# Rows of exponentials kept in DRAM and loaded spread, in place of a transpose and an exponential per target tile

## The chip, the cores and the metric

The kernel runs on one core of one Trainium2 chip. The metric is the time of one execution on the device, in microseconds. Three runs of the kernel before took 1933.40, 1940.33 and 1942.73 us; the median is 1940.33 us.

## The reference

Two graph attention layers work on 3,327 nodes with 1,024 features each and a sparse 0/1 adjacency matrix (each node has some 16 neighbours and itself). Each layer is followed by a residual sum and a layer norm:

```python
x = _layernorm(x + _L0_gnn_ref(x, adj, W, a_src, a_dst))   # 8 heads of 128
x = _layernorm(x + _L1_gnn_ref(x, adj, W, a1, a2))         # one head, relu

# layer 1
h = input @ W
f1 = h @ a1
f2 = h @ a2
e = leaky_relu(f1 + f2.T, negative_slope=0.2)
scores = where(adj > 0, e, -9e15)
attention = softmax(scores, axis=1)
h_prime = attention @ h
return relu(h_prime)
```

The weight of a source j for a target i is exp(leaky_relu(f1[i] + f2[j])). The softmax is free to scale each target's weights by a common factor, so the kernel divides by exp(0.2 f1[i]) and works with max(exp(0.8 f1[i]) * exp(f2[j]), exp(0.2 f2[j])). For each target it needs one number, exp(0.8 f1[i]), and for each source two, exp(f2[j]) and exp(0.2 f2[j]).

## The kernel before

The nodes are padded to 26 tiles of 128 (NT = 26). The program first projects all tiles for layer 0 and lists the edges of each target tile. Then one written sequence of 52 items follows, made by `pipeline`: 26 items `Layer0` and 26 items `Target` (layer 1). Under `tc.manual_schedule()` every engine runs its instructions in the order of the program text, so what stands ahead in an engine's queue is done first. Waits are set where two instructions touch the same tile.

*Blocks.* A target tile has its edges in up to five blocks: four blocks of four groups of 32 targets each, and a fifth (`EB`) for what is left over. For every block, `gather` (L1011) has POOL issue indirect DMAs (L1017), one for each group, which bring 128 source rows into one of five buffers (`near` and `src`; two further ones, `end`, for the fifth block). A target thus takes 17 gathers. `send()` issues the next gather as soon as PE has finished with the buffer it goes into.

*A target of layer 1.* `weights(b)` (L1216) makes the 128 x 128 weights of a block on DVE in three passes: the row of the target's exponentials times the source's number (L1223), the maximum with the source's other number (L1224), times the one-hot marks (L1226). The first two results lie in PSUM, in the tile `way`. `sums(b)` (L1229) multiplies the weights with the gathered rows on PE (L1235). The weights of a block are made while PE works on the block before it. `close` divides by the sum of weights on ACT and DVE. `finish` transposes the result on PE (L196, copied by ACT at L199), multiplies it with W (L1267, 32 matmuls of 512 columns) and adds the residual (L1270). `settle` is the layer norm (L217 to L224, with ACT's square root at L220) and the store to `out` (L1278). `pipeline` cuts `finish` and `settle` of the one or two targets before into steps and puts them between the blocks of the current one.

*The exponentials of the target.* The scores f1 of all nodes are in the columns `r1.s` (one column of 128 partitions for each tile), written at the end of layer 0. `Target.prepare` of the next target is called in the middle of the current target (ahead of block 2's sums, j == nb // 2). PE transposes the column, spread over 128 columns, into `way` (L1191), so that each partition holds the whole row of 128 scores; ACT makes the exponentials of it in another part of `way` (L1193), and DVE reads them from there in L1223. Then `prepare` has DVE make the marks (L1033, L1037) and SP load the target's own row of y (L1198). `own` (L1200) makes the weight of the target's own node and needs the exponentials as a column: ACT makes them at L1204, DVE uses them at L1205.

*The end of a tile of layer 0.* `Layer0.finish` normalises the tile, makes both scores (L1168), has ACT put the two exponentials of the source score into the row (L1173, L1174) and SP store it in `y_d` (L1175). The gathers of layer 1 read `y_d`.

SP issues all plain loads and stores, POOL the gathers. The 16 DMA engines carry both.

Of the kernel before, what the change touches and what calls it, by code (L numbers as in the profile page):

```python
# [9 lines left out]
F32 = mybir.dt.float32  # L10
# [3 lines left out]
AF = mybir.ActivationFunctionType  # L14
OP = mybir.AluOpType
# [4 lines left out]
P = 128  # L20
SLOPE = 0.2
# [5 lines left out]
def kernel(  # L27
# [28 lines left out]
    nc = tc.nc  # L56
    N, D = x.shape
    H, DH = a0_src.shape
    NT = (N + P - 1) // P
# [10 lines left out]
    NG = P // GT  # L70
# [37 lines left out]
    scratch = ctx.enter_context(tc.tile_pool(name="scratch", bufs=1, space=DRAM))  # L108

    ident = const.tile([P, P], F32, name="ident")  # L110
# [14 lines left out]
    idx = const.tile([P, NT, NB], I32, name="idx")  # L125
    tgt = const.tile([P, NT, NB], F32, name="tgt")
    wt1 = const.tile([P, KT, D], F32, name="wt1")
    half_d = [scratch.tile([P, D], F32, name=f"half_d{t}") for t in range(EARLY)]
    dens = const.tile([P, EARLY, H], F32, name="dens")
    io_t = const.tile([P, P], F32, name="io_t")  # L130
# [41 lines left out]
    class Phase:  # L172
# [12 lines left out]
        def bank(self, tag, shape, name, dt=F32):  # L185
            psum, bufs = self.banks[tag]
            return psum.tile(shape, dt, tag=tag, name=name, bufs=bufs)

        def sbuf(self, tag, shape, bufs, name=None, dt=F32):
            return self.pool.tile(shape, dt, tag=tag, name=name or tag, bufs=bufs)  # L190
# [319 lines left out]
    with ExitStack() as own, tc.manual_schedule():  # L510
        ph = Phase(own, "proj", {"A": 2, "T": 1})
        pool, bank = ph.pool, ph.bank
# [389 lines left out]
        tr = bank("T", [1, P], "trc")  # L902
# [50 lines left out]


    def sparse(own):
        ph = Phase(own, "sparse", {"A": 4, "S": 2, "T": 1, "E": 1})
        pool, bank, sbuf = ph.pool, ph.bank, ph.sbuf
        NS = 5
        srcs = near + [pool.tile([P, NG, HG], F32, bufs=1, name=f"src{n}") for n in range(HB, NS)]
        ends = [pool.tile([P, 1, HG], F32, bufs=1, name=f"end{n}") for n in range(2)]  # L960
        r1 = Rows(pool, 1)

        ys = [pool.tile([P, HW], F32, bufs=1, name=f"y{n}") for n in range(3)]
        for y in ys:
# [3 lines left out]
        way = bank("E", [P, HALF], "way")  # L968
# [59 lines left out]
        def marks(t):  # L1028

            m = NB - 1  # L1030
            oh = sbuf("oh", [P, m * GT + P], 2)
            parts = oh[:, : m * GT].rearrange("p (b t) -> p b t", t=GT), oh[:, m * GT :]
            nc.vector.tensor_tensor(  # L1033
                parts[0], io_t[:, :GT].unsqueeze(1).to_broadcast([P, m, GT]),
                tgt[:, t, :m].unsqueeze(2).to_broadcast([P, m, GT]), OP.is_equal,
            )
            nc.vector.tensor_scalar(parts[1], io_t, tgt[:, t, m:], None, op0=OP.is_equal)  # L1037
            return parts

        class Layer0:  # L1040
# [9 lines left out]
            def prepare(self):  # L1050
                self.re = listed.pop(self.t)
                self.oh, self.oh2 = marks(self.t)
                self.y = ys[self.n % 3]
                load_rows(self.y[:, :D], x, self.t)
                self.h = sbuf("own", [P, HW0], 2)
                nc.sync.dma_start(self.h, h0_d[self.t * P : (self.t + 1) * P, :HW0])
                if self.t < EARLY:
                    self.half = sbuf("xT", [P, KT, P], 2, "half").rearrange("p k q -> p (k q)")
                    nc.sync.dma_start(self.half, half_d[self.t])

            def own(self):

                t, h = self.t, self.h
                es = self.es = sbuf("es0", [P, H], 2)
                nc.scalar.activation(es, sd0[:, t, 0, :], AF.Exp, scale=1 - SLOPE)
                nc.vector.tensor_tensor(es, es, h[:, D : D + H], OP.mult)
                nc.vector.tensor_tensor(es, es, h[:, D + H :], OP.max)
                nc.vector.tensor_scalar(es, es, loop[:, t : t + 1], None, op0=OP.mult)
                for n in range(H):
                    d = slice(n * DH, (n + 1) * DH)  # L1070
                    if t < EARLY:
                        nc.vector.scalar_tensor_tensor(
                            h[:, d], h[:, d], es[:, n : n + 1], self.half[:, d], op0=OP.mult, op1=OP.add
                        )
                    else:
                        nc.scalar.activation(h[:, d], h[:, d], AF.Copy, scale=es[:, n : n + 1])  # L1076
                if t < EARLY:
                    nc.vector.tensor_tensor(es, es, dens[:, t, :], OP.add)
# [69 lines left out]
            def finish(self):  # L1148

                met = sbuf("met", [NG * H, P], 2)  # L1150
                nc.vector.tensor_tensor(met, self.den[: NG * H, :P], meets, OP.mult)
                nc.tensor.matmul(self.den[:, P:], met, heads, start=True, stop=True)
                yield
                ri = sbuf("ri", [P, H], 2)
                nc.vector.tensor_tensor(ri, self.den[:, P:], self.es, OP.add)
                nc.vector.reciprocal(ri, ri)
                t, row = self.t, self.y
                y = row[:, :D]
                for h in range(H):
                    yh = y[:, h * DH : (h + 1) * DH]  # L1160
                    nc.vector.scalar_tensor_tensor(
                        yh, self.acc[h // 4][:, h % 4, :], ri[:, h : h + 1], yh, op0=OP.mult, op1=OP.add
                    )
                yield
                yield from ph.norm_steps([y])
                for n in range(2):
                    pr = sbuf("pr", [P, D], 1)
                    nc.vector.scalar_tensor_tensor(  # L1168
                        pr, y, 1.0, wa[n], op0=OP.mult, op1=OP.mult, accum_out=r1.sd[:, t, n, :]
                    )  # L1170
                    if n == 0:
                        yield
                nc.scalar.activation(row[:, D + 1 : D + 2], r1.d[:, t, :], AF.Exp)  # L1173
                nc.scalar.activation(row[:, D + 2 : D + 3], r1.d[:, t, :], AF.Exp, scale=SLOPE)  # L1174
                nc.sync.dma_start(y_d[t * P : (t + 1) * P, :HW], row)  # L1175
                stored.add(t)

        class Target:
# [8 lines left out]

            def prepare(self):
                t = self.t
                tr = way[:, 3 * P :]  # L1190
                nc.tensor.transpose(tr, r1.s[:, t, :].to_broadcast([P, P]), ident)  # L1191
                self.r = way[:, ((t + 1) % 2) * P : ((t + 1) % 2 + 1) * P].rearrange("p (g t) -> p g t", g=NG)
                nc.scalar.activation(  # L1193
                    self.r.rearrange("p g t -> p (g t)"), tr, AF.Exp, scale=1 - SLOPE
                )
                self.oh, self.oh2 = marks(t)
                self.res = ys[self.n % 3]
                nc.sync.dma_start(self.res, y_d[t * P : (t + 1) * P, :HW])  # L1198

            def own(self):  # L1200

                t, res = self.t, self.res
                es = self.es = sbuf("es1", [P, 2], 2)
                nc.scalar.activation(es[:, 1:], r1.s[:, t, :], AF.Exp, scale=1 - SLOPE)  # L1204
                nc.vector.scalar_tensor_tensor(  # L1205
                    es[:, 1:], res[:, D + 1 : D + 2], es[:, 1:], res[:, D + 2 : D + 3], op0=OP.mult, op1=OP.max
                )
                nc.vector.tensor_tensor(es[:, :1], es[:, 1:], loop[:, t : t + 1], OP.mult)

# [284 lines left out]
    with arm.Else():  # L1494
        with ExitStack() as own:
            sparse(own)
# [23 lines left out]
```

## Time and profile before

| What | Value |
|---|---|
| median of three runs | 1940.33 us |
| profiled execution, its own time | 1945.79 us |
| its span, first to last instruction | 1944.1 us |
| mean granted TensorE clock | 0.918 |
| PE busy | 1633.7 us (84%) |
| DVE busy | 1184.5 us (61%) |
| ACT busy | 573.4 us (29%) |
| POOL busy | 1092.2 us (56%) |
| L1193 ACT, the exponentials of 26 rows | 262 ns each |
| L1191 PE, the transposes of 26 columns | 272 ns each |
| L1204 ACT, the exponentials of a column | 187 ns each |

Layer 0's items run until about 1190 us, layer 1's from there to the end. A profile row gives line, engine, operation and tile names, then the shapes; "<-" in brackets names what ended the idle time ahead of the instruction. An engine's busy share is a mean over stages with different limits, so the stage windows and the waits say more than the page's first line. "Granted clock" is the share of full speed that TensorE was given.

### The profile page before, as it was taken

The numbers are of one execution on the slowest core, as the hardware profiler recorded it, in microseconds if no ns is written. First come the engines' busy times: TensorE is split into PE (matmuls) and PEld (weight loads), VectorE is DVE, ScalarE is ACT, GpSimd is POOL, SyncE is SP. The second block draws the span as 40 slices with busy tenths as digits, with TensorE's granted clock in tenths as the row PEclk, the third lists the DMA queues.
The fourth block names the chain that finished last, engine by engine and source line by source line (L and its number), as shares of the span: only waits on it lengthen the run. The fifth ranks groups of instructions, "written<-read, shape, count | busy, mean of one in ns | idle before, by whom it ended". The sixth has DMA issues, their size and how long they took to land.

```text
span 1944.1 us, 35431 instructions
## 1 busy us (share of the span) xinstructions
PE 1633.7 (84%) x13168; PEld 919.9 (47%) x13168; DVE 1184.5 (61%) x3261; ACT 573.4 (29%) x1565; POOL 1092.2 (56%) x1580
## 2 busy tenths in 40 slices
PE   8699989989994777777777665798989999899988
PEld 5466556655563554554455442243434434333433
DVE  6699988777765776777777774243444344434342
ACT  5656554444321222222222121022122221222121
POOL 4433346656555666666666555565656666565640
PEclk9899999999996878888878877899999999999999
DMA  6555779887779999999999998899999999899980
GB/s 178 91 130 114 144 152 293 255 249 238 247 271 349 381 391 393 383 393 371 402 386 386 374 313 301 310 374 340 346 350 369 335 394 342 331 362 340 325 302 33
DMA packets 183364, 585.16 MB, mean 301 GB/s; under 512 B 36168, under 2 KB 42824, under 8 KB 183182
## 3 DMA queue, kind: packets, MB, share of 16 engines
q0 software_dynamic: 131056, 457.74, 68.4%
q1 hardware_dynamic: 52126, 125.06, 17.2%
q8 instruction: 107, 1.75, 0.4%
q14 instruction: 75, 0.61, 0.1%
HBM read 586.09 MB, written 51.22 MB: 328 GB/s over the span
## 4 chain that ended last, share of the span: by engine, by line
PE 43%; issue 10%; DVE 6%; ACT 4%; DMA 4%; POOL 1%; another core or an unknown queue 0%; DVEq 0%; ACTq 0%; POOLq 0%
PE mm L1267 17%; PE acc L1235 13%; PE acc L1129 8%; PE acc L1110 2%; DMA src<-h_d,idx 2%; PE tr L196 1%; ACT L1193 1%; PE acc L1118 1%; DVE e L1098 1%; ACT own L1076 1%; DMA near<-h_d,idx 1%; DVE pr L982 1%; DVE st L217 1%; ACT L220 1%; DMA src<-y_d,idx 1%
## 5 line engine op out<-in xcount | busy, mean ns | idle before, releaser
L542 PE MATMUL mm<-wt,xT 128*128 128x347 f32 (+1 forms) x1248 | 416.6, 475 | 6.8 <-ACT ht L561 3.3
L1267 PE MATMUL mm<-wt,xT 128*128 128x512 f32 x832 | 395.5, 613 | 2.6 <-issue 2.3
L1017 POOL DMA_INDIRECT src<-y_d,idx x248 | 249.1, 1005 | 166.8 <-PE acc L1235 71.0
L542 PEld LDWEIGHTS mm<-wt,xT 128*128 128x128 f32 x1248 | 228.5, 195 | 118.3 <-issue 19.7
L1017 POOL DMA_INDIRECT src<-h_d,idx x184 | 196.5, 1068 | 121.3 <-PE acc L1129 35.8
L1267 PEld LDWEIGHTS mm<-wt,xT 128*128 128x128 f32 x832 | 152.3, 193 | 211.5 <-issue 206.7
L1270 DVE SCALAR_TENSOR_TENSOR o<-mm,y 128x512 f32<-128x512 f32 x52 | 36.0, 692 | 322.2 <-PE acc L1235 126.4
L1017 POOL DMA_INDIRECT near<-y_d,idx x168 | 169.5, 1009 | 108.7 <-PE acc L1235 48.3
L1129 PE MATMUL acc<-src,e 128*32 128x128 f32 x2944 | 161.3, 324 | 52.1 <-issue 47.5
L1017 POOL DMA_INDIRECT near<-h_d,idx x120 | 130.6, 1088 | 82.4 <-PE acc L1129 31.0
L1235 PE MATMUL acc<-src,es 128*32 128x341 f32 x1488 | 130.6, 485 | 41.8 <-DVE es L1226 31.8
L1129 PEld LDWEIGHTS acc<-src,e 128*32 128x32 f32 x2944 | 111.5, 130 | 113.4 <-issue 93.8
L1098 DVE TENSOR_TENSOR e<-oh,way 128x1024 f32<-128x1024 f32 x104 | 127.1, 1222 | 59.3 <-ACT w L1096 43.1
L1129 PE MATMUL acc<-near,e 128*32 128x128 f32 x2048 | 116.0, 333 | 48.7 <-issue 34.8
L199 ACT ACTIVATE xT<-tr 128x512 f32<-128x512 f32 x104 | 62.1, 598 | 299.9 <-PE tr L196 151.6
L1129 PEld LDWEIGHTS acc<-near,e 128*32 128x32 f32 x2048 | 79.7, 133 | 93.7 <-issue 84.4
L1096 ACT ACTIVATE w<-way 128x32 f32<-128x32 f32 x104 | 20.3, 195 | 351.4 <-DVE way L1094 186.6
L1249 ACT ACTIVATE z<-y,ri 128x342 f32<-128x342 f32 (+1 forms) x78 | 39.5, 569 | 277.0 <-issue 121.6
L1235 PE MATMUL acc<-near,es 128*32 128x342 f32 (+1 forms) x1008 | 85.8, 469 | 21.3 <-DVE es L1226 14.0
L629 POOL DMA_INDIRECT near<-h_d,idx x76 | 82.1, 1080 | 31.5 <-issue 22.9
L1235 PEld LDWEIGHTS acc<-src,es 128*32 128x32 f32 x1488 | 44.4, 114 | 115.0 <-issue 61.1
L346 ACT ACTIVATE junk<-ad 128x1664 uint8<-128x1664 uint8 x52 | 83.8, 1611 | 16.2 <-POOL ad L342 14.8
(242 smaller groups left out, 2587.8 us busy)
## 6 DMA issues: line engine op xcount, KB each, us to landing
h_d<-ht SPq DMA_DIRECT2D x26, 520.0 KB
own<-h_d SPq DMA_DIRECT2D x26, 520.0 KB
y_d<-y SPq DMA_DIRECT2D x26, 514.0 KB
y<-y_d SPq DMA_DIRECT2D x26, 514.0 KB
x<-in_x_dram SPq DMA_DIRECT2D x25, 512.0 KB
y<-in_x_dram SPq DMA_DIRECT2D x25, 512.0 KB
out_dram<-o SPq DMA_DIRECT2D x25, 512.0 KB
ad<-in_adj_dram POOLq DMA_DIRECT2D x25, 415.9 KB
```

What stands on the lines that cost most here:

```text
L199: nc.scalar.activation(part, tr, AF.Copy)
L346: nc.scalar.activation(junk, ad[:, n * THR : (n + 1) * THR], AF.Copy, accum_out=self.d[:, n : n + 1])
L542: nc.tensor.matmul(acc, xT[t][:, k, :], wt[:, k, CUTS0[c] : CUTS0[c + 1]], start=k == 0, stop=k == KT - 1)
L629: nc.gpsimd.indirect_dma_start(out=src[n % 3][:, g, :], out_offset=None, in_=h0_d[:THR, :], in_offset=bass.IndirectOffsetOnAxis(ap=idx[:, ...
L1017: nc.gpsimd.indirect_dma_start(out=s[:, g, :w], out_offset=None, in_=table[:n, :], in_offset=bass.IndirectOffsetOnAxis(ap=idx[:, t, b * NG ...
L1098: nc.vector.tensor_tensor(e, oh.unsqueeze(2).to_broadcast([P, ng, H, wide]), wp.unsqueeze(3).to_broadcast([P, ng, H, wide]), OP.mult,)
L1110: nc.tensor.matmul(self.acc[j - 1].rearrange("p h d -> p (h d)"), ident, self.h[:, (j - 1) * HALF : j * HALF], start=False, stop=False,)
L1129: nc.tensor.matmul(self.acc[h // 4][g * GT : (g + 1) * GT, h % 4, :], e[:, g, h, :], rowsof[:, g, h, :], start=first and h % 4 == 0, stop= ...
L1235: nc.tensor.matmul(self.acc[c][to, :m], es[:, g, :], s[:, g, CUTS[c] : CUTS[c + 1]], start=b == 0, stop=b == EB,)
L1249: nc.scalar.activation(z[:, cut], self.res[:, cut], AF.Copy, scale=ri[:, 1:2])
L1267: nc.tensor.matmul(acc, xT[:, k, :], wt1[:, k, half], start=k == 0, stop=k == KT - 1)
L1270: nc.vector.scalar_tensor_tensor(o[:, half], acc, 0.0, res[:, half], op0=OP.max, op1=OP.add)
```

## The change

At the end of a tile of layer 0, ACT makes the exponentials of the target score as a column too, in a column of the new tile `grow`, and SP stores these 128 numbers in a DRAM tile of their own (`row_d[t]`), one number from each partition. `Target.prepare` has no transpose and no exponential left: SP loads the 128 numbers into all 128 partitions of a new SBUF tile `rr` (two buffers), each partition reading the same 512 bytes. `own` reads the column from `grow`. The row of exponentials so lies in SBUF where it lay in PSUM.

```diff
+    row_d = [scratch.tile([1, P], F32, name=f"row_d{t}") for t in range(NT)]
...
+        grow = pool.tile([P, NT], F32, bufs=1, name="grow")
...
                 nc.scalar.activation(row[:, D + 1 : D + 2], r1.d[:, t, :], AF.Exp)
                 nc.scalar.activation(row[:, D + 2 : D + 3], r1.d[:, t, :], AF.Exp, scale=SLOPE)
+                nc.scalar.activation(grow[:, t : t + 1], r1.s[:, t, :], AF.Exp, scale=1 - SLOPE)
                 nc.sync.dma_start(y_d[t * P : (t + 1) * P, :HW], row)
+                to = row_d[t][:, :]
+                nc.sync.dma_start(
+                    bass.AP(tensor=to.tensor, offset=to.offset, ap=[[1, P], [1, 1]]), grow[:, t : t + 1]
+                )
...
             def prepare(self):
                 t = self.t
-                tr = way[:, 3 * P :]
-                nc.tensor.transpose(tr, r1.s[:, t, :].to_broadcast([P, P]), ident)
-                self.r = way[:, ((t + 1) % 2) * P : ((t + 1) % 2 + 1) * P].rearrange("p (g t) -> p g t", g=NG)
-                nc.scalar.activation(
-                    self.r.rearrange("p g t -> p (g t)"), tr, AF.Exp, scale=1 - SLOPE
+                self.r = sbuf("rr", [P, P], 2).rearrange("p (g t) -> p g t", g=NG)
+                of = row_d[t][:, :]
+                nc.sync.dma_start(
+                    self.r.rearrange("p g t -> p (g t)"),
+                    bass.AP(tensor=of.tensor, offset=of.offset, ap=[[0, P], [1, P]]),
                 )
...
                 es = self.es = sbuf("es1", [P, 2], 2)
-                nc.scalar.activation(es[:, 1:], r1.s[:, t, :], AF.Exp, scale=1 - SLOPE)
                 nc.vector.scalar_tensor_tensor(
-                    es[:, 1:], res[:, D + 1 : D + 2], es[:, 1:], res[:, D + 2 : D + 3], op0=OP.mult, op1=OP.max
+                    es[:, 1:], res[:, D + 1 : D + 2], grow[:, t : t + 1], res[:, D + 2 : D + 3], op0=OP.mult, op1=OP.max
                 )
```

## The prediction

> **What bounds the kernel now.** I read the page first (shares by engine), then the windows by stage, then the waits of layer 1 and last the timeline of one target in it. The page has PE busy for 84% of the span, but its busy rows are not the limit everywhere. The windows, whose columns are stretch, length, busy us of PE, PEld, DVE, ACT and POOL, granted clock, DMA share and GB/s, separate the stages:
>
> ```profile
> 660.00:1180.00 520.00, 387.89 (x5228) 259.50 (x5220) 383.22 (x1005) 120.67 (x331) 323.11 (x304) 0.84 0.99 379
> 1276.73:1881.22 604.49, 557.18 (x3147) 238.85 (x3147) 244.57 (x727) 128.42 (x220) 376.85 (x376) 0.98 0.94 350
> 1441.92:1466.67 24.75, 24.75 (x147) 10.78 (x151) 11.89 (x36) 5.84 (x10) 14.94 (x15) 1.00 0.88 325
> 1548.70:1602.85 54.15, 49.47 (x287) 21.35 (x287) 22.21 (x66) 11.67 (x20) 35.93 (x37) 1.00 1.01 393
> ```
>
> The first is layer 0: the DMA engines are full (0.99), PE is not. The second is layer 1, 22 targets at 604.49/22 = 27.48 us each: PE is busy for 557.18 and idle for 47.3, and the DMA engines have 6% left. The third is the one target in which PE never waits: 24.75 us. What ends PE's idle time between 1276 and 1882 is in the waits (total us, times, longest):
>
> ```profile
> DVE way L1223 <- ACT way L1193: 53.2, 16, 3.4
> PE acc L1235 <- DVE es L1226: 44.6, 19, 2.8
> ```
>
> PE waits for DVE's weights, and DVE for ACT's exponentials at L1193. One occurrence, in the timeline:
>
> ```profile
> 1517.55 0.60 ACT L199 ACTIVATE xT<-tr 128x512 f32<-128x512 f32 x1 [7.18 <-PE mm L1267]
> 1518.17 1.28 ACT L220 ACT_TABLE_LOAD   x1
> 1519.46 0.20 ACT L220 ACTIVATE sg<-sg 128x1 f32<-128x1 f32 x1
> 1519.68 1.28 ACT L1193 ACT_TABLE_LOAD   x1
> 1520.98 0.26 ACT L1193 ACTIVATE way<-way 128x128 f32<-128x128 f32 x1
> ...
> 1516.96 0.68 DVE L1033 TENSOR_TENSOR oh<-io_t,tgt 128x512 f32<-128x512 f32 x1
> 1517.56 0.28 DVE L1037 TENSOR_SCALAR oh<-io_t,tgt 128x128 f32<-128x128 f32 x1
> 1521.27 0.30 DVE L1223 TENSOR_TENSOR way<-way,near 128x128 f32<-128x128 f32 x1 [3.44 <-ACT way L1193]
> ...
> 1515.86 3.70 PE L1267 MATMUL mm<-wt,xT 128*128 128x512 f32 x8
> 1522.28 3.59 PE L1235 MATMUL acc<-near,es 128*32 128x341 f32 x24 [2.73 <-DVE way L1224]
> ```
>
> ACT swaps its function table twice per target, for the square root (L220) and back for the exponential. DVE starts 0.03 us after ACT ends, though this L1223 makes block 3 of the current target and L1193 makes the row of the next one: both lie in the tile "way", so the wait is on the tile, not on the value. PE then stands for 2.73 us, and its next 24 matmuls take 3.59 us where 1.93 is usual, at half clock.
>
> **Removed.** (1) L1193, the last use of that tile by ACT, and with L1204 the last exponential of layer 1. The square root then finds its table loaded, so 22 + 22 loads of 1.28 us go in this window; ACT is 21% busy (128.42 of 604.49), so that time by itself is worth nothing. What counts is that L1223 no longer follows ACT. In the occurrence above DVE is free at 1517.84; 0.30 + 0.30 + 0.29 us of work with the gaps of the rows give the weights at about 1518.85, and PE needs them at 1519.56. Next late is DVE's own chain, with 0.7 us to spare. PE's period falls to the third window's 24.75: 22 x (27.48 - 24.75) = 60.0 us, of which 47.3 is idle time and 557.18 - 22 x 24.75 = 12.7 is half clock. To it come 1.5 us (the stall at 1276.73, before the window) and 1.4 us (half clock behind the stall at 1881.22).
> (2) L1191 on PE, 0.27 us, of which little is exposed: from the four transposes to the sums behind them is 0.64 us start to start with it and 0.53 without; 26 x 0.11 = 2.9 us. PE's side in all: 60.0 + 1.5 + 1.4 + 2.9 = 65.8 us.
>
> **Added.** (3) In layer 0 one more ACT exponential per tile, 0.19 us like L1174, behind what the store of y waits for; ACT is 23% busy there. DVE at L1205 reads the stored column and waits for nothing new. (4) Per tile a store of 128 words on SP's queue, behind the store of y and ahead of the next tile's loads: an issue of 0.32 us on a queue that issues about five times in some 20 us. These are 128 packets per tile in a stage whose DMA is full. The nearest rows are loads of 4-byte words between 252 and 256 us, and one 544-byte set between 341 and 342 (packets, MB, share of 16 engines):
>
> ```profile
> q1 hardware_dynamic: 1233, 0.00, 17.3%
> q1 hardware_dynamic: 144, 0.07, 23.8%
> ```
>
> The first gives 0.173 x 16 x 4.0/1233 = 9 ns each: 26 x 128 x 9/16 = 1.9 us. No row shows a store of single words; the far bound is the page's mean packet of that queue, 0.172 x 16 x 1944.1/52126 = 103 ns, which makes 21 us. I take 2, since size is what the price follows in the two lines. (5) Per target a load of 128 packets of 512 bytes; the second line, 0.24 us of all engines, gives 26 x 0.24 = 6.2 us, 5.2 in the window. On SP it stands ahead of the load of y and behind the out store of the tile before. It waits only for that and for the buffer of the target before last: it can go out at about 1496 for weights made at 1530. The row y_d to y goes out at 1515.47 and is needed by 1533.67, without a wait shown. Cover: some 20 us; beyond that each us of lateness is a us of PE. (6) The row now lies in SBUF, so L1223 reads two SBUF operands. DVE L1033 reads two as well, and POOL's issue beside it took the usual time, while a fast single-operand pass stretched one:
>
> ```profile
> 1516.73 0.99 POOL L1017 DMA_INDIRECT src<-y_d,idx  x1 [0.31 <-issue]
> 1522.09 1.18 POOL L1017 DMA_INDIRECT src<-y_d,idx  x1 [0.30 <-DVE way L1224]
> ```
>
> So nothing (no gain either: DVE's passes L1223 to L1226 take 0.29 to 0.30 us wherever their operands lie), with an upper bound of the whole of L1223: 5 x 0.30 = 1.5 us of POOL per target. POOL's work is 17 x 1.30 = 22.1 us per target, so even 23.6 stays under 24.75. The Trainium skill (GPSIMD Engine Reference, Specifications) says that GpSimd's SBUF interfaces meet contention from Vector instructions with two SBUF inputs; by it the upper bound would hold. This trace shows none beside L1033.
>
> **What limits the gain: the gathers.** The 22 periods moved 350 GB/s. At layer 0's sustained 379 they take 604.49 x 350/379 = 558 us, at the 393 of the fourth window 538, at share 1.00 of their own mix 568; with the added rows (5.2) that saves 41, 61 or 31 us. On top comes the lead: the last gather is issued at 1883.80, its sums start at 1912.59, 28.8 us later, of which about 6 is transfer (issue stops at 1503.87, the engines' share drops after 1509). Up to 23 us may be used up over the layer: DMA's side allows 54 to 84 us, PE's side 65.8 - 1.9 = 64. Two limits so near each other rarely both hold in full, since each slip of one stalls the other; I take 55, DMA's low end.
> The Trainium skill (DMA: Bandwidth & Descriptors, Specifications) puts the HBM limit of one core at about 358 GB/s, which speaks against the change: as an estimate, 604.49 x 350/358 = 591 us, a saving of 13 us before the lead. The 379 over 520 us in the first window is above that, so the measurement decides.
>
> **Sum.** The profiled execution took 1945.79 us, with a span of 1944.1 and 1.7 around it: 1945.79 - 55 = 1891. It stands 5.5 above the median shown, 1940.33, so I forecast 1940.33 - 55 = 1885.
>
> **Rivals.**
> B. The gathers bound layer 1 from the start and no lead is used: saving 31 to 41, 1899 to 1909. For it: share 0.99 and 1.01 in whole stretches already. Against: in the unstalled target it is 0.88, and POOL waits 94 us (56.0 + 38.3) for PE to free buffers, so transfers aren't what PE waits for.
> C. DVE's chain takes the stall's place. It has 0.7 us; if L1270 ahead of it comes 2 us later, half the stall is back: saving about 30 less little, 1905 to 1922. For it: L1270 itself waits for PE, in the same order as before.
> D. The change doesn't do what it says: another wait on ACT or on the loaded row ends at the same time. Then only L1191's 2.9 less 1.9 is left: 1935 to 1945. Against: the 0.03 us between L1193 and L1223.
> E. Slower: PE, now in step with the gathers, idles often in short pieces and falls to half clock, as in layer 0, where the mean is 0.84. At that clock 24.64 us of work take 29.3, 1.85 more than now: + 41 us, 1981. It decides where layer 1's mean clock falls under 24.64/27.48 = 0.90. For it: after the gather wait of 8 us at 1236 PE ran slowly until 1257. Against: PE had 25% idle in layer 0 and would have some 5% here.
>
> **How the numbers follow.** My forecast 0.55 (own range 1872 to 1898), B 0.20, C 0.13, D 0.05, E 0.07. Range 1868 (PE's side with all of DMA's) to 1922 (C's end), leaving out D, E and a little more. About 0.5%, 10 us, is what this kernel's measurement tells from no change: faster is A, B and C, 0.88; same 0.05; slower 0.07.
>
> **What would show it.** Right: no table loads in layer 1 but one, no wait of L1223 on ACT, periods of 25 to 25.5 us, DMA share 0.98 or more, a few waits of L1223 on gathers late in the layer. Wrong: periods above 27, a mean clock under 0.9, L1223 waiting on the load of the row, or layer 0 longer by more than 5 us.

## The result, and the profile after

The changed kernel is slower. Six runs took 2010.01 to 2023.93 us with a median of 2013.69; beside them, six runs of the kernel before took 1927.85 to 1953.39 with a median of 1941.53. The ratio is 1.038, with a 95% interval of 1.033 to 1.043 (the medians alone give 1.037). The forecast was 1885 us, with a range up to 1922 and a chance of 0.07 for slower.

The profiled execution took 2017.74 us, with a span of 2015.4 us: 71.3 us more span than before. Where layer 1's sums begin divides it. These are the first rows of the sums line before (L1235) and after (L1241); behind the duration stand the first and last start:

```profile
L1235 PE MATMUL acc<-src,es x1488: 447/451/779, 1198.0 to 1899.0; 128*32 128x342 f32 x124, 128*32 128x341 f32 x62
```

```profile
L1241 PE MATMUL acc<-src,es x1488: 447/451/779, 1311.7 to 1970.0; 128*32 128x342 f32 x111, 128*32 128x341 f32 x75
```

What comes ahead of layer 1's sums grew by 1311.7 - 1198.0 = 113.7 us; what follows shrank from 1944.1 - 1198.0 = 746.1 to 2015.4 - 1311.7 = 703.7, by 42.4 us. The gain is there, and a loss more than twice as large stands in front of it. The stage windows of the changed kernel (columns as in the prediction) show both:

```profile
660.00:1180.00 520.00, 332.35 (x4372) 232.39 (x4366) 318.53 (x832) 100.23 (x291) 261.32 (x252) 0.75 1.01 311
1311.70:1394.30 82.60, 55.91 (x333) 20.71 (x333) 22.39 (x72) 6.91 (x12) 46.52 (x47) 0.82 0.85 296
1394.30:1952.90 558.60, 556.42 (x3125) 243.28 (x3124) 242.28 (x727) 63.72 (x132) 372.44 (x374) 1.00 1.00 381
```

The last line is layer 1's 22 regular targets: 558.60/22 = 25.39 us each, where they took 27.48 before. PE is idle for 2.2 us of them (before: 47.3) at a clock of 1.00, and ACT's busy time has halved. The groups by line on ACT show why. L221, L220 before, is the square root of the layer norm of both layers: its loads went from 50 to 27, one for each tile of layer 0 and one more at 1391.69 us, ahead of the regular targets. The 23 loads of the exponential in layer 1 (L1193) are gone. First two rows of the kernel before, then all loads of the changed kernel:

```profile
L220 ACT ACT_TABLE_LOAD x50 | 64.2, 1283 | 1.0
L1193 ACT ACT_TABLE_LOAD x23 | 29.5, 1283 | 0.4
```

```profile
L221 ACT ACT_TABLE_LOAD x27 | 34.6, 1283 | 0.8 <-issue 0.4
L1175 ACT ACT_TABLE_LOAD x26 | 33.4, 1283 | 0.6 <-issue 0.2
L200 ACT ACT_TABLE_LOAD x1 | 1.3, 1283 | 0.8 <-PEq L1514 0.8
```

The first line of the stage windows is the loss. In layer 0 the DMA engines are as full as before (1.01 against 0.99), but move 311 GB/s where they moved 379. One tile shows how. Its word store is issued at 702.85 us; these are windows of 2 us:

```profile
706.00:708.00 2.00, 0.18 (x1) 0.18 (x2) 1.41 (x2) 0.32 (x2) 1.21 (x2) 0.83 1.00 409
708.00:710.00 2.00, 2.00 (x4) 0.81 (x4) 1.63 (x4) 0.20 (x1) 0.99 (x1) 0.50 1.06 409
710.00:712.00 2.00, 2.00 (x33) 1.54 (x36) 1.93 (x9) 0.00 (x0) 0.00 (x0) 0.50 1.28 80
712.00:714.00 2.00, 2.00 (x42) 1.80 (x35) 1.30 (x4) 0.00 (x0) 0.00 (x0) 0.50 0.94 84
714.00:716.00 2.00, 2.00 (x22) 1.01 (x24) 0.00 (x0) 0.00 (x0) 0.99 (x1) 0.96 1.35 136
716.00:718.00 2.00, 0.89 (x24) 0.47 (x17) 0.00 (x0) 0.00 (x0) 0.84 (x1) 1.00 1.23 162
718.00:720.00 2.00, 0.57 (x3) 0.25 (x3) 0.00 (x0) 0.00 (x0) 1.14 (x2) 1.00 0.28 64
720.00:722.00 2.00, 0.94 (x10) 0.51 (x13) 0.40 (x2) 0.05 (x1) 0.00 (x0) 0.75 0.99 385
```

Read the last two columns together. Up to 710 us the 16 engines are full and move 409 GB/s. For the next 8 us they are booked as full or more and move 80 to 162, then they are nearly idle for 2 us, and at 720 they are back at 385. Packets are open all the while and hardly end. They are not the store's own: its packets of 4 bytes start between 708.2 and 710.1 us and are recorded with 9 ns each. The gathers' packets of 4,160 bytes, nearly all of which take 161 ns between 700 and 708 us, are held up behind them: of the 208 that start between 710 and 718 us a quarter take 0.94 us or more, the longest 4.75. Over the tiles the loss is 113.7/26 = 4.4 us per tile. A share of 1.00 thus says that packets are under way, not that bytes are moving; only the GB/s beside it shows the stall.

The last such store also stands in the turn from layer 0 to layer 1. Layer 1's gathers read what was stored just ahead of it, and the profile names the store of the words as the end of POOL's wait:

```profile
1311.07 0.32 SPq L1178 DMA_DIRECT2D y_d<-y  x1
1311.48 0.38 SPq L1180 DMA_DIRECT2D row_d<-grow  x1
1311.92 0.78 SPq L1199 DMA_DIRECT2D rr<-row_d  x1
1320.78 0.98 POOL L1019 DMA_INDIRECT src<-y_d,idx  x1 [23.71 <-DMA row_d<-grow]
```

POOL starts 9.7 us after that tile's store of y was issued. Before the change it was 1201.18 - 1197.37 = 3.8 us, and what ended the wait there was PE, not a store:

```profile
1201.18 0.99 POOL L1017 DMA_INDIRECT src<-y_d,idx  x1 [14.12 <-PE acc L1235]
```

### The profile page after: what moved, and what is told of

Same layout as the page of the kernel before. It is cut to its first block, busy times and chain, and to the rows that moved or that the text cites. A ratio compares the mean times of both kernels' runs of the same rounds, so it can differ in the third digit from the quotient of the medians.

```text
span 2015.4 us, 35459 instructions
## 1 busy us (share of the span) xinstructions
PE 1639.4 (81%) x13142; PEld 940.2 (47%) x13142; DVE 1184.0 (59%) x3261; ACT 506.5 (25%) x1493; POOL 1081.3 (54%) x1580
## 4 chain that ended last, share of the span: by engine, by line
PE 41%; DMA 17%; issue 6%; DVE 4%; POOL 1%; ACT 1%; SPq 0%; DVEq 0%; another core or an unknown queue 0%; POOLq 0%; ACTq 0%
PE mm L1273 18%; PE acc L1241 12%; DMA src<-h_d,idx 10%; PE acc L1131 5%; DMA near<-h_d,idx 2%; PE acc L1112 2%; DMA end<-h_d,idx 2%; PE acc L1120 1%; DMA own<-h_d 1%; PE tr L197 1%; DVE e L1100 1%; DVE pr L984 1%; POOL src L1019 1%; DMA src<-y_d,idx 1%; DMA half<-half_d 1%
## 5 line engine op out<-in xcount | busy, mean ns | idle before, releaser
L1019 POOL DMA_INDIRECT src<-h_d,idx x184 | 189.7, 1031 | 204.2 <-PE acc L1131 72.0
L1131 PEld LDWEIGHTS acc<-src,e 128*32 128x32 f32 x2944 | 120.5, 143 | 147.8 <-issue 84.0
L1241 PE MATMUL acc<-src,es 128*32 128x341 f32 x1488 | 135.6, 468 | 27.9 <-DVE es L1232 15.1
L1131 PE MATMUL acc<-near,e 128*32 128x128 f32 x2048 | 106.1, 337 | 62.3 <-issue 38.9
L1241 PEld LDWEIGHTS acc<-src,es 128*32 128x32 f32 x1488 | 50.6, 112 | 102.7 <-issue 65.6
L1241 PE MATMUL acc<-near,es 128*32 128x342 f32 (+1 forms) x1008 | 86.3, 455 | 3.8 <-issue 3.5
```

The source lines that it names most:

```text
L1019: nc.gpsimd.indirect_dma_start(out=s[:, g, :w], out_offset=None, in_=table[:n, :], in_offset=bass.IndirectOffsetOnAxis(ap=idx[:, t, b * NG ...
L1131: nc.tensor.matmul(self.acc[h // 4][g * GT : (g + 1) * GT, h % 4, :], e[:, g, h, :], rowsof[:, g, h, :], start=first and h % 4 == 0, stop= ...
L1241: nc.tensor.matmul(self.acc[c][to, :m], es[:, g, :], s[:, g, CUTS[c] : CUTS[c + 1]], start=b == 0, stop=b == EB,)
```

## The experiments

The runs fell on several chips, and the kernel before doesn't take the same time on all: 1829 to 1830 us on two (called kind X here), 1928 to 1942 us on the others, the one of the result among them (kind Y). Every ratio below is against the kernel before on the same chip. A price in microseconds belongs to its kind; where two kinds are set side by side, the text says so.

| Kernel | Kind | Median us, before beside it | Ratio, 95% interval |
|---|---|---|---|
| e1_store_only | X | 1991.35, 1829.40 | 1.0873, 1.0855 to 1.0891 |
| e2_turn_grow | X | 1828.92, 1829.40 | 1.0000, 0.9988 to 1.0012 |
| e3_row_store | X | 1832.85, 1829.40 | 1.0010, 0.9997 to 1.0024 |
| e4_apart_64 | X | 1833.40 (one run), 1829.40 | |
| e5_after_again | X | 2000.35, 1829.87 | 1.0917, 1.0889 to 1.0945 |
| e6_before_again | X | 1832.18, 1829.87 | 1.0007, 0.9994 to 1.0019 |
| e7_load_words | X | 1833.36, 1829.87 | 1.0011, 0.9997 to 1.0025 |
| e8_apart_16 | X | 1839.98, 1829.87 | 1.0052, 1.0034 to 1.0071 |
| e9_apart_8 | Y | 1948.78, 1928.52 | 1.0122, 1.0053 to 1.0191 |
| e10_sbuf_words | Y | 1935.00, 1928.52 | 1.0026, 0.9982 to 1.0070 |
| e11_turn_again | Y | 1900.17, 1928.52 | 0.9858, 0.9805 to 0.9911 |
| e12_row_again | Y | 1904.27, 1928.52 | 0.9886, 0.9830 to 0.9941 |
| e13_copy | Y | 1891.79, 1932.06 | 0.9802, 0.9756 to 0.9848 |
| e14_load | Y | 1937.96, 1932.06 | 1.0030, 0.9982 to 1.0078 |
| e15_turn_load | Y | 1894.64, 1932.06 | 0.9828, 0.9778 to 0.9877 |

### Is it the store alone?

e1 is the kernel before with only the new exponential and the word store; nothing reads the stored words.

```diff
                 nc.scalar.activation(row[:, D + 2 : D + 3], r1.d[:, t, :], AF.Exp, scale=SLOPE)
+                nc.scalar.activation(grow[:, t : t + 1], r1.s[:, t, :], AF.Exp, scale=1 - SLOPE)
                 nc.sync.dma_start(y_d[t * P : (t + 1) * P, :HW], row)
+                to = row_d[t][:, :]
+                nc.sync.dma_start(
+                    bass.AP(tensor=to.tensor, offset=to.offset, ap=[[1, P], [1, 1]]), grow[:, t : t + 1]
+                )
```

> The kernel before with only the first half of the change: ACT makes the column, SP stores its 128 words; nothing reads them, layer 1 stays as it was. In the profiles layer 0 ended (first sums of layer 1) at 1198 us before and at 1312 after, 114 us later, and layer 1 took 746 before and 704 after, 42 less. Theory 'words' (the store of single words holds up the DMA engines): layer 0 ends near 1312, layer 1 takes 746, 2050 to 2060 in all. Theory 'load' (the loss comes from the spread loads or from layer 1's other order): as before, 1940.

It cost 1991.35 - 1829.40 = 162 us. The absolute time expected was off, because the chip's kernel before is faster; the ratio is on the side of the store. Its windows of layer 0 and of layer 1, and between them layer 0 of the kernel before on kind X (from e6 below):

```profile
660.00:1150.00 490.00, 277.96 (x3971) 210.81 (x3970) 288.81 (x748) 92.67 (x268) 238.24 (x227) 0.72 1.01 302
660.00:1150.00 490.00, 334.40 (x5063) 252.66 (x5063) 378.20 (x981) 117.84 (x319) 311.13 (x296) 0.75 1.01 393
1350.00:1750.00 400.00, 397.82 (x2305) 172.65 (x2297) 174.85 (x522) 90.54 (x157) 287.40 (x285) 1.00 1.01 397
```

Layer 0 moves 302 GB/s at a full share, much as the changed kernel's 311, where the kernel before moves 393; layer 1, where no word is stored, moves 397. So the loss needs neither the spread load nor layer 1's new order, and e2 below shows that the added exponential costs nothing. That the price is 162 us here and 113.7 in the traces of the first chip lies mostly in the kernel before: with the store, layer 1's sums begin at 1311.5 us here and at 1311.7 there; without it at 1162.0 (e6) and 1198.0.

### The same values without the word store

e2 keeps the columns in SBUF and lets PE turn them in layer 1, straight into the place that DVE reads; no DRAM, and no exponential in layer 1.

```diff
-                tr = way[:, 3 * P :]
-                nc.tensor.transpose(tr, r1.s[:, t, :].to_broadcast([P, P]), ident)
-                self.r = way[:, ((t + 1) % 2) * P : ((t + 1) % 2 + 1) * P].rearrange("p (g t) -> p g t", g=NG)
-                nc.scalar.activation(
-                    self.r.rearrange("p g t -> p (g t)"), tr, AF.Exp, scale=1 - SLOPE
-                )
+                tr = way[:, ((t + 1) % 2) * P : ((t + 1) % 2 + 1) * P]
+                nc.tensor.transpose(tr, grow[:, t : t + 1].to_broadcast([P, P]), ident)
+                self.r = tr.rearrange("p (g t) -> p g t", g=NG)
```

> The column of exponentials is made at the end of a tile of layer 0 as in the change, but there is no store and no load: PE turns the column into the tile way and DVE reads it there, with no ACT in between. Theory 'words', and any other that puts the loss into the added transfers: layer 0 ends near 1198, layer 1 takes 690 to 704, 1888 to 1902 in all. Theory 'ACT' (the added exponential in layer 0 costs): layer 0 ends near 1312, 2000 to 2016.

e3 is the changed kernel with its spread load, but PE turns the column in layer 0, ACT copies the row out, and the store is one row of 512 bytes from one partition.

```diff
+                tr = bank("T", [P, 4, P], "tr")
+                nc.tensor.transpose(tr[:1, 0, :], grow[:, t : t + 1], ident)
+                line = sbuf("line", [1, P], 2)
+                nc.scalar.activation(line, tr[:1, 0, :], AF.Copy)
+                nc.sync.dma_start(row_d[t], line)
```

> The changed kernel, but PE turns the finished column into one row of 128 words on one partition, ACT copies it, and SP stores these 512 bytes in one piece; the spread load stays. Theory 'words': layer 0 ends near 1200, layer 1 takes 700, 1895 to 1910 in all. Theory 'extra transfer' (any further transfer at that place of SP's queue, in a stage whose DMA is full, costs 4.4 us per tile) and theory 'place' (the new DRAM tiles move the others): 2005 to 2015, as the changed kernel.

On kind X neither loses (1.000 and 1.001), so the spread load and the row's way through DRAM cost nothing that shows (e3's interval ends at 1.0024). Neither gains either; that opened the second question, below. On kind Y the same two kernels were run again:

> The kernel that makes the exponentials in layer 0, keeps the columns in SBUF and lets the TensorE turn them in layer 1, again: no store and no exponential in layer 1. Theory 'late signals': on a chip where the kernel before takes about 1829 us it takes the same (ratio 0.998 to 1.002, 24.68 us a target); on one where the kernel before takes about 1940 us, layer 1 falls from 27.5 to about 25.4 us a target and the whole to 1885 to 1905 us (ratio 0.97 to 0.982). Rival 'no gain anywhere without the spread load': ratio 1.00 on both.

> The changed kernel, with the column turned on the TensorE in layer 0 and stored as one row of 512 bytes, again. Theory 'words': the store was the whole loss, so on a chip where the kernel before takes about 1829 us it takes the same (ratio 0.999 to 1.003), and on one where it takes about 1940 us it keeps the gain that was forecast for layer 1: 1885 to 1905 us (ratio 0.97 to 0.982). Rival 'the row through DRAM costs by itself': 1.01 or more on both.

Both gain, 0.986 and 0.989, at 1900 and 1904 us within the 1885 to 1905 expected; the ratios show a little less gain than the expected 0.97 to 0.982, because the kernel before took 1928.5 us and not 1940. e11's 22 regular targets take (1834.5 - 1275.9)/22 = 25.39 us, the same as in the changed kernel. So with the store mended, the change does on a chip like the first what it was forecast to do, at about half the size.

### What about the words is it?

e4 stores the same 128 words 64 bytes apart; e8 and e9 store them 16 and 8 bytes apart (4 and 2 in place of the 16 below).

```diff
+    row_d = [scratch.tile([P, 16], F32, name=f"row_d{t}") for t in range(NT)]
...
+                nc.sync.dma_start(row_d[t][:, :1], grow[:, t : t + 1])
```

> As the first kernel (store only, not read), but the 128 words go 64 bytes apart in DRAM. Theory 'same bytes' (the words of a store hinder each other because they lie in the same few lines of memory): layer 0 ends near 1200, 1940 to 1950 in all. Theory 'small write' (each write of 4 bytes costs by itself, wherever it lies): layer 0 ends near 1312, 2050 to 2060.

> The kernel before, with the exponentials stored as 128 words 16 bytes apart in DRAM (4 in each 64 bytes, 2,048 bytes in all), unread. Adjacent words (16 in each 64 bytes) cost 162 us, words 64 bytes apart 4 us. Theory 'a turn for each word of a line': the cost goes with the words that share 64 bytes, 4 of 16: 30 to 50 us more (ratio 1.016 to 1.028). Rival 'any sharing': a line that two writers share costs in full: 140 to 170 us. Rival 'the row of 512 bytes is what counts': 32 words in 512 bytes against 8 at 64 bytes apart, so still a quarter of the full price, and then the words 64 bytes apart must show a tenth of it: 30 to 50 us here as well.

> The kernel before, with the exponentials stored as 128 words 8 bytes apart in DRAM (8 in each 64 bytes, 1,024 bytes in all), unread. Adjacent words (16 in 64 bytes) cost 162 us, 16 bytes apart (4 in 64 bytes) 10 us, 64 bytes apart (1) 4 us. Theory 'a turn for each pair of writers of a line': the cost goes with the square of the words that share 64 bytes, and 8 of 16 cost a quarter: 35 to 50 us more (ratio 1.019 to 1.027). Rival 'a threshold between 4 and 16': nearly the whole 162 us, or nearly nothing.

With the words 64 bytes apart the windows behind a store (here issued at 707.2 us) have no hole:

```profile
708.00:710.00 2.00, 0.00 (x0) 0.00 (x0) 1.97 (x8) 0.00 (x0) 1.24 (x2) 0.98 1.02 407
710.00:712.00 2.00, 0.00 (x0) 0.00 (x0) 1.32 (x4) 0.20 (x1) 1.69 (x2) 0.50 1.02 400
712.00:714.00 2.00, 1.43 (x3) 1.00 (x4) 1.25 (x6) 0.00 (x0) 1.02 (x2) 0.50 1.01 369
714.00:716.00 2.00, 2.00 (x22) 0.84 (x24) 2.00 (x8) 0.00 (x0) 1.35 (x2) 0.50 1.02 395
716.00:718.00 2.00, 2.00 (x56) 1.93 (x48) 1.64 (x5) 0.96 (x2) 1.61 (x2) 0.82 0.99 404
```

It is the same number of packets of the same size, so neither the size nor the count is the price: it is how near together they land. The prices are 162 us adjacent (16 words in 64 bytes), 10 at 16 bytes (4 words) and 4 in a single run at 64, all on kind X, and 20 at 8 bytes apart (8 words, interval 10 to 37) on kind Y. The price falls faster than in proportion. On kind X a quarter of 162 would be 40, and 10 was measured. On kind Y adjacent words cost 113.7 us in the first chip's traces; half of that would be 57, above e9's interval. "A turn for each pair" gives 162/16 = 10 and 113.7/4 = 28, and both fit (in e9's trace layer 1's sums begin at 1223.9 us, 26 behind the 1198.0 of the kernel before); e9's expectation of 35 to 50 was worked out from kind X's 162. The steep shape is shown; with two points the law stays open.

Two runs ask for the direction and the place. e7 loads 128 adjacent words from DRAM after each tile; e10 sends the column by the same 128 packets into one row of SBUF.

```diff
+                nc.sync.dma_start(
+                    word[:, t : t + 1], bass.AP(tensor=x.tensor, offset=x.offset + t * D, ap=[[1, P], [1, 1]])
+                )
```

> The kernel before, with a load of 128 adjacent words (one to each partition, from the first 512 bytes of the tile's first row of x) behind each store of a tile, unread: as many packets of 4 bytes as the store had, to as few lines of DRAM, in the other direction. Theory 'writes': a word written has to be merged into a line that the next word needs as well, and reads don't: within 10 us of the kernel before (ratio 0.995 to 1.006). Rival 'any access': words that share their lines queue whichever way they go, or 128 packets of one word do: 140 to 170 us more where the store alone cost 162 us (ratio 1.07 to 1.09).

```diff
+                nc.sync.dma_start(sbuf("line", [1, P], 2), grow[:, t : t + 1])
```

> The kernel before, with the column of exponentials sent by the same 128 packets of 4 bytes into one row of SBUF (512 adjacent bytes of one partition) where the change sends it to DRAM, unread. Theory 'a line of DRAM is merged for each word': SBUF takes words one by one, so nothing: ratio 0.997 to 1.004. Rival 'adjacent words from 16 queues collide wherever they land': 140 to 170 us more (ratio 1.075 to 1.09).

Neither costs anything that shows (1.001 and 1.003, each interval holding 1). So it takes all three: writes, into DRAM, of words next to each other. That the memory merges each word into a line that the next word needs too would fit this, but no run looks inside, and it stays an explanation.

The Trainium skill (DMA: Bandwidth & Descriptors, Specifications) says that transfers under 512 bytes miss line rate, and that the engine reads, modifies and writes below that size. These runs can't look inside the engine. Words 64 bytes apart are as far under 512 bytes as adjacent ones and cost 4 us in their one run where adjacent words cost 162: the nearness sets this price, not the size alone.

### Where the gain of layer 1 lives

e5 and e6 are the two kernels as they stand, both on a chip of kind X.

> The changed kernel again, beside the kernel before on the same chip. Theory 'words': all of its loss is the store of 128 adjacent words, and layer 1 gains only where the TensorE stalls on ScalarE. Where the kernel before takes about 1829 us, as beside the last four kernels, layer 1 has nothing to gain (24.68 us a target with ScalarE's table loads and without them), so the changed kernel costs what the store alone cost: 1985 to 1997 us. Where the kernel before takes about 1940 us, it costs 2010 to 2025 us. Rival 'the gain is real everywhere': some 40 us of gain in layer 1 here too, which gives 1950 us beside 1829 us.

> The kernel before, for a profile on this chip. Theory 'late signals': its layer 1 is 27.5 us a target only where TensorE's completion signals come late to ScalarE and VectorE; where the whole takes about 1829 us, layer 1 takes 24.7 us a target with all of its table loads still there, ScalarE's second copy of the source rows starts right behind the transposes, and layer 0 ends near 1160 us. Rival 'the table loads themselves stall the TensorE': 27 us a target here too, and the difference in the total lies in layer 0 alone. Ratio 1.000 in both.

The changed kernel on kind X loses 2000.35 - 1829.87 = 170 us, a little above e1's price. The profiles divide it: layer 1's sums begin at 1317.8 and, in the kernel before, at 1162.0, 155.8 us apart or 6.0 per tile; the first target of layer 1 takes 14 us longer (77.7 against 63.6 us to the first output). The regular targets take (1935.9 - 1395.5)/22 = 24.56 us against 24.68, so next to nothing is won there. The kernel before has all its table loads on this chip, and yet:

```profile
1225.60:1768.60 543.00, 543.00 (x3150) 235.89 (x3154) 245.33 (x728) 128.41 (x220) 382.42 (x383) 1.00 1.01 396
```

22 targets at 24.68 us and PE not idle for a moment, with ACT exactly as busy (128.41 us) as on the first chip (128.42), where PE idled 47.3. One target in the timeline of e6, at the same place within a target as the occurrence shown in the prediction:

```profile
1515.55 0.60 PE L196 MATMUL tr<-ident,z 128*128 128x128 f32 x4
...
1516.19 0.60 ACT L199 ACTIVATE xT<-tr 128x512 f32<-128x512 f32 x1 [3.62 <-PE tr L196]
1516.80 1.28 ACT L220 ACT_TABLE_LOAD   x1
1518.10 0.20 ACT L220 ACTIVATE sg<-sg 128x1 f32<-128x1 f32 x1
1518.33 1.28 ACT L1193 ACT_TABLE_LOAD   x1
1519.62 0.26 ACT L1193 ACTIVATE way<-way 128x128 f32<-128x128 f32 x1
1519.91 0.30 DVE L1223 TENSOR_TENSOR way<-way,src 128x128 f32<-128x128 f32 x1 [1.02 <-ACT way L1193]
...
1520.58 0.29 DVE L1226 TENSOR_TENSOR es<-way,oh 128x128 f32<-128x128 f32 x1
1521.68 1.93 PE L1235 MATMUL acc<-src,es 128*32 128x341 f32 x24
```

The chain is the one that the prediction read, loads and wait included. But ACT's copy starts 0.04 us after the four transposes end, at 1516.15, and the weights are there at 1520.87, 0.81 us before PE turns to them. In the first chip's occurrence the same transposes ended at 1513.95 and the copy began at 1517.55, 3.60 us later; the two loads then end too late:

```profile
1513.35 0.60 PE L196 MATMUL tr<-ident,z 128*128 128x128 f32 x4
```

The other targets agree. In e6 this second copy starts 0.04 us after its transposes in all 26 targets. In the trace of the kernel before it is on time (0.04 us) in 3 of 26, one of them the prediction's target without a wait, and 0.6 to 3.7 us late in the others. In its regular targets, all but one, PE's idle time ahead of the next sums is that delay less some 0.87 us: 2.21 us late gives 1.34 idle, 2.79 gives 1.92, 3.60 gives 2.73, and 0.77 gives none (the one: 0.88 late, 0.36 idle). So the loads cost only where ACT starts late. Why it starts late on kind Y no run tells: the program is the same, and the trace names signals of PE for the wait.

e13 takes away only the loads. The transposes and the two instructions stay, with copies for exponentials.

```diff
                 nc.scalar.activation(
-                    self.r.rearrange("p g t -> p (g t)"), tr, AF.Exp, scale=1 - SLOPE
+                    self.r.rearrange("p g t -> p (g t)"), tr, AF.Copy, scale=1 - SLOPE
                 )
...
-                nc.scalar.activation(es[:, 1:], r1.s[:, t, :], AF.Exp, scale=1 - SLOPE)
+                nc.scalar.activation(es[:, 1:], r1.s[:, t, :], AF.Copy, scale=1 - SLOPE)
```

> The kernel before with both exponentials of layer 1 computed as plain copies (the exponential function is left out, so its weights are other numbers); the transposes, the instructions and their waits stay, and ScalarE has only square roots and copies in layer 1, so no table to change. Where the kernel before takes about 1930 us: theory 'table loads' says that the loads alone make 26.5 to 27.5 us a target, so this falls to 25.4 as without the exponentials (ratio 0.98 to 0.989); rival 'ScalarE's place in the chain of waits' says that it stays at 26.5 to 27.5 (ratio 0.995 to 1.005). Where the kernel before takes about 1829 us, both say 24.7 us a target and 0.998 to 1.002.

0.980, and (1826.3 - 1268.0)/22 = 25.38 us a target: all that the removal of both exponentials brings. In its timeline ACT still starts late, 1.92 us after the transposes end at 1516.35, but the weights are ready at 1520.29, ahead of PE's sums at 1521.88:

```profile
1515.75 0.60 PE L196 MATMUL tr<-ident,z 128*128 128x128 f32 x4
1516.18 0.27 PE L1191 MATMUL way<-ident,sd 128*128 128x128 f32 x1
1518.27 0.60 ACT L199 ACTIVATE xT<-tr 128x512 f32<-128x512 f32 x1 [5.50 <-PE acc L1235]
1518.76 0.19 ACT L220 ACTIVATE sg<-sg 128x1 f32<-128x1 f32 x1
1519.04 0.26 ACT L1193 ACTIVATE way<-way 128x128 f32<-128x128 f32 x1
1519.33 0.30 DVE L1223 TENSOR_TENSOR way<-way,src 128x128 f32<-128x128 f32 x1 [0.27 <-issue]
...
1520.00 0.29 DVE L1226 TENSOR_TENSOR es<-way,oh 128x128 f32<-128x128 f32 x1
...
1521.88 2.62 PE L1235 MATMUL acc<-src,es 128*32 128x341 f32 x24
```

So the price of the exponentials on kind Y was the loads, not the transposes and not the instructions on the shared tile.

The last row shows something else: these 24 matmuls take 2.62 us where e6's take 1.93. In the changed kernel and in e11, e12, e13 and e15, all on kind Y, the fourth of a target's full blocks (the one behind this place) is slow in nearly every target: from its first matmul to PE's next work it takes 2.46 to 2.59 us by each run's median, against 1.86 in the three other blocks. In e2, e5 and e6, on kind X, it takes 1.86 us too. These 0.6 to 0.7 us are about the difference between 25.4 and 24.7 us a target.

The last pair asks whether the kinds differ by what their transfers reach: 393 GB/s on X and 380 on Y in layer 0. Both kernels, before and e2, get 393 kB more to load per target of layer 1, unread. Both runs fell on kind Y, so what they were expected to show on kind X is not tested.

```diff
                 nc.sync.dma_start(self.res, y_d[t * P : (t + 1) * P, :HW])
+                nc.sync.dma_start(spare, x[min(t, NT - 2) * P : (min(t, NT - 2) + 1) * P, :768])
```

> The kernel before with a load of 128 packets of 3,072 bytes per target of layer 1, unread: 393 kB beside the 9.7 MB that 24.68 us at 394 GB/s make, 4% more traffic in layer 1 alone. Theory 'transfer rate': the chips differ in what the transfers reach under load (394 and 380 GB/s), and transfers that come later leave no slack for ScalarE's table loads: on a chip where the kernel before takes 1829 us, layer 1 goes from 24.7 to between 26.5 and 27.5 us a target, as on the other chips, and the whole to 1876 to 1902 us (ratio 1.026 to 1.040); on one where it takes 1930 us, 27.5 to 28.5 us a target (ratio 1.01 to 1.027). Rival 'only the TensorE's signals differ': no more than the transfer itself, 26 x 1.0 us: at most 1855 us (ratio at most 1.014).

> The kernel with columns of exponentials kept in SBUF and turned by the TensorE (no store, no exponential in layer 1), with the same extra load of 393 kB per target of layer 1. Theory 'transfer rate': without table loads layer 1 goes at the transfers' pace, 25.7 us a target on a chip where the kernel before takes 1829 us, so about 1855 us (ratio 1.012 to 1.016), 20 us or more under the kernel before with the same load; on a chip where it takes 1930 us, 26.4 us a target and about 1926 us (ratio 0.99 to 1.005), 20 us or more under the kernel before with the load. Rival 'only the signals differ': within 5 us of the kernel before with the load where that one takes about 1829 us without it.

For kind Y my theory was wrong. The load cost the kernel before nothing that can be told from zero (1.003, interval 0.998 to 1.008), and e15, at 0.983, has nothing to show for it either: its targets take (1827.8 - 1268.6)/22 = 25.42 us where e11 took 25.39. The windows of layer 1, e11's first:

```profile
1420.00:1760.00 340.00, 339.16 (x1924) 149.68 (x1924) 148.57 (x444) 38.61 (x80) 226.37 (x228) 1.00 0.99 377
1420.00:1760.00 340.00, 339.26 (x1903) 151.40 (x1902) 145.56 (x438) 38.84 (x80) 225.27 (x226) 1.00 1.01 393
```

In e15 the DMA engines move 393 GB/s where e11 moved 377 in the same window at a share of 0.99, and the pace is the same. So the transfers' rate doesn't bound layer 1 on kind Y, though their share says full. Why the fourth block is slower there is still open, like the late start.

The turned column (e11) and the row stored in one piece (e12) beat both kernels on kind Y; on kind X (e2 and e3) they equal the kernel before.

## Why the prediction was wrong, step by step

**(4), the word store: this is the step that failed.** It was put at 1.9 us, with a far bound of 21, "since size is what the price follows". Measured: 113.7 us in the traces of the first chip, 162 us alone on kind X, 60 to 85 times the value taken and 5 to 8 times the far bound. Both bounds were prices of packets that the trace before shows: loads of words, and mean packets of the queue. The direction was taken as not mattering; e7 shows that a load of adjacent words really is free, so the row was right for what it priced and was carried to something else. I also saw the price as engine time of the store's own packets, shared by 16. That time was right, 9 ns a packet in the changed kernel's trace; the loss is in the other transfers, whose packets last up to 4.75 us behind such a store, and the sum had no term for that. The bound should have had an end for "the trace has no store of this kind", and a chance to go with it.

**(1), the removal: right in mechanism, smaller in size.** In the regular targets no table load is left, the first pass of the weights no longer waits for ACT, and the period fell, by e13 because of the loads. The period came to 25.39, not 24.75: 22 x (27.48 - 25.39) = 46 us in place of 60. PE's one clean target was taken for all of them, and the slow fourth block was not foreseen. The 27.48 was one execution, too: e9 and e10, which have the kernel before's layer 1 on kind Y, have periods of 26.18 and 26.47 us (e14, with its unread load, 27.47). From the first two the same 25.39 saves 17 and 24 us, and the medians of e11 and e12 gave 28 and 24. The start of layer 1 gave nothing (82.6 us from the first sums to the first output, 79.6 before) in place of 1.5 saved.

**(2), the transposes of the score: nothing on kind Y.** e13 keeps them and reaches 25.38 us; the 2.9 us weren't there. On kind X, where PE is never idle, the changed kernel is 24.68 - 24.56 = 0.12 us a target faster, about the 0.11 that was priced.

**(3) and (6): right.** e2 and e3 have the extra exponential in layer 0 and cost nothing by it on kind X. DVE's first pass on the SBUF row took 294 to 296 ns by its shapes, and no target was paced by POOL (372.44 us busy of 558.60).

**(5), the spread load: right in that it costs PE nothing.** Nothing in the waits stands behind the loaded row, and e3 and e12 contain it. The 6.2 us that it was to take from the gathers' gain don't show: e12, with the load, has (1838.9 - 1281.2)/22 = 25.35 us a target, e11, without it, 25.39.

**What limits the gain.** The gathers were named as the limit, at 54 us, and the net taken was 55; the 22 periods gave 46 and the whole of layer 1 42.4. The size is near by luck, since the reason was wrong: e15 moves 4% more at the same pace. The range's low end, 1868, doesn't follow from the terms either: PE's side of 64 us gives 1940.33 - 64 = 1876.

**The rivals.** B and C would have been layer 1's cases; without the store the changed kernel would have taken 2013.69 - 113.7 = 1900 us, in B's range, but e12 saved 24 us and e11 28, which from 1940.33 is 1916 and 1912, in C's. Neither mechanism is what the runs show: the transfers were not the limit (e15), and L1270 on DVE did not bring the stall back, since PE is idle for 2.2 us in the 22 targets together. E had the right sign and the wrong mechanism: layer 1's clock is 1.00. That layer 0 could be longer by more than 5 us was named as what would make the prediction wrong, and it is what happened; no rival was built on it.

## What to carry to other kernels

Don't store a column of single words as an adjacent row in DRAM: turn it on the TensorE and store one row, or leave it in SBUF and turn it where it is read; words spread 64 bytes apart cost 4 us here, in one run. When a price is taken from the nearest row, check that it agrees in direction, place and neighbourhood as well as in size, and keep the far end open where no row agrees. Read the share of the DMA engines only together with the GB/s: the share was 1.01 in the stage that lost a fifth of its throughput.

## What was not expected of the hardware

- A store of 512 bytes as 128 adjacent words holds up the core's other transfers: 409 GB/s fell to 80 to 162 for 8 us, at shares of 0.94 to 1.35. As many words to SBUF (1.003), as loads (1.001), or 64 bytes apart (4 us, one run) cost nothing that can be told from zero.
- The same kernel takes 1829 us on two chips and 1928 to 1942 us on the others. In the two traces of the kernel before, 36 us of it are in front of layer 1's sums (1162.0 and 1198.0), where layer 0's transfers moved 393 and 381 GB/s, and 78 us behind them (668 and 746), where ACT's second copy followed the transposes after 0.04 us in all 26 targets of one and 0.6 to 3.7 us late in 23 of 26 of the other. The changed kernel's regular targets are 0.8 to 2.1 us shorter on the slower kind (against e9 and the kernel before) and 0.12 on the faster.
- 377 GB/s at a share of 0.99 was not the limit in layer 1: with more to load it became 393 GB/s in the same time.
